# The end of the last batch: bias by a product, residual straight from PSUM, normalisation of three quarters on ScalarE

## The chip, the cores and the metric

The kernel runs on one core of a Trainium2 chip. The metric is device time in microseconds (us) of one whole execution; lower is better. In the profile PE is TensorE (matmuls), PEld its weight loads, DVE is VectorE, ACT is ScalarE, POOL is GpSimd and SP the engine that issues nearly all DMAs. A suffix q (SPq, POOLq) is the sequencer of that engine.

## The reference

Two layers are applied to x, of shape 16 batches x 1024 nodes x 256 channels, in 32-bit floats. Layer 0 is an attention over the nodes (4 heads) whose queries are mixed through the adjacency; layer 1 is two graph convolutions. After each comes a layer norm of the input plus the layer's result. What matters here is the end of layer 1:

```python
def _graph_conv(x, adj, w_loop, w_neigh, b):
    loop = jnp.einsum('bnd,dh->bnh', x, w_loop)
    neigh = jnp.einsum('nm,bmh->bnh', adj, jnp.einsum('bnd,dh->bnh', x, w_neigh))
    return loop + neigh + b
h = jax.nn.relu(_graph_conv(x, adj, w1_loop, w1_neigh, b1))
h = jax.nn.relu(_graph_conv(h, adj, w2_loop, w2_neigh, b2))
return (x + h) * 0.5
...
x = _layernorm(x + _L1_gnn_ref(x, adj, ...), axis=-1)
```

Since x + (x + h)/2 is 1.5 (x + h/3), and a layer norm takes out a common factor, the kernel computes x + h/3: the weights w2 and the bias b2 are divided by three once, at the start, and the norm's epsilon is divided by 2.25 (`EPS2`). The input b2 is a row of 256 numbers; in these inputs it is zero, but the kernel adds it like any other.

## The kernel before

A batch is 1024 nodes, kept as 8 tiles of 128 nodes (partitions) by 256 channels. Through the main loop, batch b's attention runs beside the graph convolutions of batches b-1 and b-2 (class `Joined`, which does two convolutions' adjacency products together) and the norm of b-3. Order is written out by hand: each engine executes its instructions in the order in which the Python code emits them (`tc.manual_schedule()`), with semaphores for data and for buffers that are used again. Only the small check behind it (the lines from 1145 on: whether every softmax denominator stayed in range) is put in place by a scheduler. If that check fails, a slower safe version would run; it does not run here.

After the loop, batches 12 to 15 are finished. The last lines of `run()` do, in this order: the norm and store of batch 12, those of batch 13, `c2.last()` and `c2.moments()` for batch 14, and then `c1.ending(...)` for batch 15, into which the rest of batch 14 is put as `aside`.

`ending` (lines 817 to 841) works on quarters: 2 tiles of 128 nodes each, 512 columns. `second` (line 768) forms u, the neighbour sums of h1 with the adjacency, in two halves of 512 nodes: 8 products of 128x512 each, then a copy from PSUM to SBUF on ACT (`uT`, line 777). Quarters 0 and 1 need the first half of u only, and are put into the middle of the second half; quarters 2 and 3 follow it. A quarter in the kernel before is:

- PE, `outer` (lines 782 and 783): per tile one product with `w2n_sb` and one with `w2l_sb`, summed in PSUM, so four products of 128x256 a quarter. An f32 product shows as two MATMUL instructions in the profile (x2).
- DVE, `residual` (lines 787 and 790): z = PSUM + b2 (128x512), then x = max(z, 0) + x.
- DVE, `statistics` (lines 278 and 279): per tile BN_STATS and BN_AGGR, giving mean and variance.
- DVE and POOL, `reciprocal_deviation` (lines 283 and 284): variance + eps, then the power -1/2 on POOL, which works on a 128x2 piece.
- DVE, `leave` of the quarter before (lines 290 and 825): `normalize` subtracts the mean and multiplies, two instructions of 128x256, and SP stores 256 KB to the output.

So the DVE queue reads z, x, statistics, rstd of quarter g, and then the normalisation of quarter g-1; the last quarter's normalisation comes alone at the end. `rstd`, `mv_e` and the PSUM tiles of one bank have two buffers each, so that a quarter uses again what the one two before it used. Batch 14's norm, `finish_aside` (lines 811 and 813), is already done on ACT: a shift of -mean x rstd is made on DVE, and eight activations x rstd + shift (128x256) follow on ACT.

Of the kernel before, what the change touches and what calls it, by code (L numbers as in the profile page):

```python
# [10 lines left out]
F32 = mybir.dt.float32  # L11
I32 = mybir.dt.int32
AF = mybir.ActivationFunctionType
ALU = mybir.AluOpType
# [4 lines left out]
def kernel(  # L19
# [31 lines left out]
    nc = tc.nc  # L51

    B, N, C = x.shape
    P = 128
# [22 lines left out]
    const = ctx.enter_context(tc.tile_pool(name="const", bufs=1))  # L77
    xpool = ctx.enter_context(tc.tile_pool(name="xpool", bufs=3))
    work = ctx.enter_context(tc.tile_pool(name="work", bufs=1))
    small = ctx.enter_context(tc.tile_pool(name="small", bufs=4))  # L80
# [43 lines left out]
    w2n_sb = const.tile([HID, C], F32, name="w2n_sb")  # L124
    b1_sb = const.tile([HID, 1], F32, name="b1_sb")
    b2_sb = const.tile([P, C], F32, name="b2_sb")
# [30 lines left out]
    nc.gpsimd.memset(neg_half, -0.5)  # L157
    ones_sb = const.tile([P, 1], F32, name="ones_sb")
    nc.gpsimd.memset(ones_sb, 1.0)

    fold = const.tile([P, Q, S], F32, name="fold")
    nc.vector.tensor_reduce(fold[:, 0, :], ident.rearrange("p (i k) -> p k i", k=S), AX.X, ALU.add)
# [112 lines left out]
    def statistics(mv, xb, ts_, name):  # L275
        for t in ts_:
            st = small.tile([P, nc.vector.BN_STATS_DIM], F32, tag="st", name=f"st_{name}_{t}")
            nc.vector.bn_stats(st, xb[:, t, :])
            nc.vector.bn_aggr(mv[:, t, :], st)

    def reciprocal_deviation(mv, name, eps, count=NT):
        rstd = small.tile([P, NT], F32, tag="rstd", name=f"rstd_{name}", bufs=2)[:, 0:count]
        nc.vector.tensor_scalar_add(rstd, mv[:, :, 1], eps)
        nc.gpsimd.tensor_tensor(rstd, rstd, neg_half[:, 0:count], ALU.pow)
        return rstd

    def normalize(mv, rstd, xb, count=NT):

        for t in range(count):
            nc.vector.tensor_scalar(xb[:, t, :], xb[:, t, :], mv[:, t, 0:1], rstd[:, t:t + 1],  # L290
                                    op0=ALU.subtract, op1=ALU.mult)
# [407 lines left out]
    class GraphConv:  # L699
# [76 lines left out]
                self.neighbours(j, pu, range(TJ, NT), rows01)  # L776
                nc.scalar.copy(self.uT[:, ts(j, FB)], pu)

        def outer(self, g, per, p2):
            for i in range(per):  # L780
                t = g * per + i
                nc.tensor.matmul(p2[:, ts(i, C)], self.uT[:, ts(t, P)], w2n_sb, start=True, stop=False)  # L782
                nc.tensor.matmul(p2[:, ts(i, C)], self.h1T[:, ts(t, P)], w2l_sb, start=False, stop=True)  # L783

        def residual(self, g, per, p2):
# [31 lines left out]
        def ending(self, dst, rows01, aside):  # L817

            per = FB // C
            parts = []  # L820

            def leave(g, mv, rstd):
                rows = self.x[:, g * per:(g + 1) * per, :]
                normalize(mv, rstd, rows, per)
                nc.sync.dma_start(out=dst[g * per * P:(g + 1) * per * P, :].rearrange("(t p) c -> p t c", p=P), in_=rows)

            def quarter(g):
                p2 = (bank_psum if g % 2 else half_psum)(f"h2e_ps_{g}")
                self.outer(g, per, p2)
                self.residual(g, per, p2)  # L830
                mv = small.tile([P, per, 2], F32, tag="mv_e", name=f"mv_e_{g}", bufs=2)
                statistics(mv, self.x[:, g * per:(g + 1) * per, :], range(per), f"e{g}")
                rstd = reciprocal_deviation(mv, f"e{g}", EPS2, per)
                if parts:
                    leave(*parts.pop())
                parts.append((g, mv, rstd))

            self.second(rows01, lambda: (aside(), quarter(0), quarter(1)))
            quarter(2)
            quarter(3)  # L840
            leave(*parts.pop())

    class Joined:

# [365 lines left out]
```

## Time and profile before

| what | us |
|---|---|
| median of three runs | 2174.52 |
| the three runs | 2174.29, 2174.52, 2175.86 |
| time of the profiled execution | 2174.29 |
| its span (first to last instruction) | 2172.4 |
| PE busy in the span | 2155.6 (99%) |
| DVE busy | 1893.7 (87%) |
| ACT busy | 1027.7 (47%) |
| POOL busy | 368.2 (17%) |
| stretch from the first product of quarter 0 to the last normalisation | 2150.35 to 2167.80 |

The span and the time of the same execution differ by 1.89 us, which lies outside the first and last instruction. The busy shares are of the whole span. The part that the change touches is the last 22 us of it, so shares over the whole say little of it; the chain of waits and the timeline of that stretch say more. In the chain a row is a start time, a length and what ran; "issue" is time in which the engine waited for nothing that the profile shows. In the groups a row is line, engine, operation, output and inputs, shapes, count, busy time, mean time of one in ns, and the idle time just before it.

### The profile page before, as it was taken

To read this page: it belongs to the slowest core of one execution; us is meant where nothing else is said; L and a number is where in the kernel's file an instruction comes from. 1 tells how busy PE (TensorE), PEld (TensorE's weight loads), DVE (VectorE), ACT (ScalarE), POOL (GpSimd) and SP (SyncE) were. 2 spreads that over 40 slices of the span, in tenths; PEclk is the share of its full clock that TensorE was granted. 3 is DMA by queue.
4 is the path that set the end of the run, shared out by engine and by line. 5 is a ranking of instruction groups with operands and counts; after the bars stand their busy time and mean duration, and the time that the engine had idled before them with its cause. 6 is when DMAs were issued, how large, how long until landed. Compare 5 with 4: busy or idle time off the path is not lost.

```text
span 2172.4 us, 23124 instructions
## 1 busy us (share of the span) xinstructions
PE 2155.6 (99%) x8054; PEld 1026.6 (47%) x8054; DVE 1893.7 (87%) x2431; ACT 1027.7 (47%) x1346; POOL 368.2 (17%) x210
## 2 busy tenths in 40 slices
PE   9999999999999999999999999999999999999997
PEld 5344444544444444444444445454454544544354
DVE  4978988898998989989899898999989899898965
ACT  4744545535455453445444454445543445535411
POOL 1011120221303113031120301203022130221021
PEclk9999999999999999999999999999999999999999
DMA  9393563746557374583655626556374653743342
GB/s 230 95 139 116 140 175 89 119 153 122 149 125 144 124 121 155 125 164 102 113 158 130 163 88 114 172 122 155 97 111 166 121 155 113 121 149 82 117 138 96
DMA packets 610619, 286.22 MB, mean 132 GB/s; under 512 B 504640, under 2 KB 569024, under 8 KB 610496
## 3 DMA queue, kind: packets, MB, share of 16 engines
q1 hardware_dynamic: 610224, 284.15, 55.0%
q8 instruction: 65, 1.06, 0.2%
q14 instruction: 58, 0.48, 0.1%
q10 hardware_dynamic: 272, 0.52, 0.1%
HBM read 238.16 MB, written 46.46 MB: 131 GB/s over the span
## 4 chain that ended last, share of the span: by engine, by line
PE 97%; DVE 2%; ACT 0%; DMA 0%; issue 0%; SPq 0%; POOLq 0%; DVEq 0%; POOL 0%
PE s L596 20%; PE av L616 20%; PE hu_ps L875 17%; PE g_ps L549 16%; PE v_ps L363 5%; PE k_ps L408 4%; PE t_ps L714 3%; PE h_ps L782 3%; PE hu_ps L721 2%; PE g_ps L476 2%; PE h_ps L783 2%; DVE acc L605 1%; PE h_ps L736 1%; PE u_ps L765 1%; PE k_ps L353 1%; PE den_ps L628 0%
## 5 line engine op out<-in xcount | busy, mean ns | idle before, releaser
L599 ACT ACTIVATE pr<-s 128x1024 f32<-128x1024 f32 x512 | 476.4, 1054 | 180.0 <-PE s L596 179.9
L605 DVE TENSOR_TENSOR acc<-acc,pr 128x1024 f32<-128x1024 f32 x384 | 494.4, 1288 | 40.7 <-DVE acc L605 0.5
L596 PE MATMUL s<-qT,kT 64*128 64x512 f32 x2048 | 458.8, 598 | 0.7 <-ACT qT L483 0.7
L616 PE MATMUL av<-pr,v 128*64 128x512 f32 x2048 | 453.6, 595 | 0.0
L596 PEld LDWEIGHTS s<-qT,kT 64*128 64x128 f32 x2048 | 191.8, 186 | 237.1 <-ACT pr L599 109.5
L616 PEld LDWEIGHTS av<-pr,v 128*64 128x64 f32 x2048 | 141.4, 137 | 300.0 <-issue 283.9
L329 POOL TENSOR_TENSOR rstd<-rstd,neg_half 128x32 f32<-128x32 f32 x16 | 87.1, 5441 | 1108.6 <-DVE rstd L327 1108.6
L462 ACT ACTIVATE wg<-c_row,c_col 128x1024 f32<-128x1024 f32 x128 | 147.0, 1148 | 73.0 <-DVE accB L607 54.2
L468 DVE SCALAR_TENSOR_TENSOR wg<-wg,adj 128x1024 f32<-128x1024 f32 x128 | 149.9, 1211 | 13.8 <-ACT wg L463 13.8
L875 PE MATMUL hu_ps<-adj,R 128*128 128x512 f32 x360 | 158.3, 596 | 0.0
L463 ACT ACTIVATE wg<-wg 128x1024 f32<-128x1024 f32 x128 | 135.4, 1058 | 4.1
L317 ACT ACTIVATE sq<-xB_a 128x1024 f32<-128x1024 f32 x32 | 33.8, 1057 | 190.0 <-DVE xB_a L312 188.8
L363 PE MATMUL v_ps<-kvw_sb,xT 128*128 128x256 f32 x512 | 120.2, 379 | 0.1
L549 PE MATMUL g_ps<-wg,S 128*128 128x512 f32 x224 | 116.7, 603 | 0.0
L363 PEld LDWEIGHTS v_ps<-kvw_sb,xT 128*128 128x128 f32 x512 | 97.2, 190 | 38.4 <-issue 21.0
L549 PE MATMUL g_ps<-T,S 128*128 128x512 f32 x224 | 114.4, 592 | 0.0
L549 PE MATMUL g_ps<-wg,x 128*128 128x512 f32 x224 | 109.0, 599 | 0.0
L875 PE MATMUL hu_ps<-adjT,t 128*128 128x512 f32 x240 | 105.7, 592 | 0.0
L875 PEld LDWEIGHTS hu_ps<-adj,R 128*128 128x128 f32 x360 | 67.3, 190 | 78.9 <-issue 76.8
L603 DVE TENSOR_TENSOR acc<-pr,pr 128x1024 f32<-128x1024 f32 x64 | 76.9, 1201 | 24.1 <-ACT pr L599 24.1
L607 DVE STREAM_TRANSPOSE accB<-acc 128x1024 f32<-128x1024 f32 x64 | 79.7, 1245 | 3.1
L609 DVE TENSOR_REDUCE den_part<-accB 128x32 f32<-128x1024 f32 x64 | 78.1, 1220 | 2.2
(187 smaller groups left out, 2862.7 us busy)
## 6 DMA issues: line engine op xcount, KB each, us to landing
adj<-in_adj_dram SPq DMA_DIRECT2D x128, 512.0 KB, 4.7
adj<-adjT SPq DMA_DIRECT2D x120, 512.0 KB, 10.2
para<-in_L_gnn_para_dram SPq DMA_DIRECT2D x32, 512.0 KB, 3.5
xB_a<-in_x_dram SPq DMA_DIRECT2D x128, 128.0 KB, 4.2
x1d<-xB_a SPq DMA_DIRECT2D x128, 128.0 KB, 3.4
x<-x1d SPq DMA_DIRECT2D x16, 1024.0 KB, 16.9
xB<-in_x_dram SPq DMA_DIRECT2D x120, 128.0 KB, 4.4
x<-in_x_dram SPq DMA_DIRECT2D x15, 1024.0 KB, 7.3
```

Source lines behind the costliest of these rows:

```text
L329: nc.gpsimd.tensor_tensor(self.rstd, self.rstd, neg_half, ALU.pow)
L363: nc.tensor.matmul(pv[:, ts(i, C)], xT[:, cc, ts(g * per + i, P)], kvw_sb[:, cc, C:2 * C], start=(cc == 0), stop=(cc == NC - 1))
L408: nc.tensor.matmul(dst, self.a[n], self.w[n], start=not again, stop=True, skip_group_check=again)
L462: nc.scalar.activation(wg, self.c_row, AF.Abs, bias=self.c_col[:, t:t + 1], scale=-1.0)
L463: nc.scalar.activation(wg, wg, AF.Tanh, scale=-0.5)
L468: nc.vector.scalar_tensor_tensor(wg, wg, 1.0, self.adj.pop(t), op0=ALU.add, op1=ALU.mult)
L549: nc.tensor.matmul(self.p[n], x_n[:, k, :], w_n, start=(k == 0), stop=(k == TJ - 1))
L596: nc.tensor.matmul(ps[:, ts(s, FB)], self.kT[rows, pair, ts(mt, P)], self.qT[rows, pair, ts(j, FB)], start=True, stop=True)
L599: nc.scalar.activation(pr, ps, AF.Exp)
L605: nc.vector.tensor_add(acc, acc, pr)
L616: nc.tensor.matmul(pav[s * HD:(s + 1) * HD, :], self.v[:, mt, pair * P + s * HD:pair * P + (s + 1) * HD], self.pr[mt][:, ts(s, FB)], start ...
L875: nc.tensor.matmul(dst, self.x[n][:, k, :], half_adj[w][:, k, :] if w else of_rows(rows, k), start=(start and k == 0), stop=(k == TJ - 1), ...
```

## The change

A row of 128 ones (`ones_row`, one partition) is made at the start. In `ending`:

- `outer` is called with `bias=True`: each tile's sum in PSUM begins with a product of the row of ones and the row of b2, contracted over one partition, ahead of the two products it had. That is two more products of 128x256 a quarter, eight in all.
- `residual` is no longer called there. One operation of DVE reads PSUM, takes the maximum with 0 and adds x.
- `leave` has two forms. For quarters 0, 1 and 2 a shift (128x2) is made on DVE, and two activations on ACT form x rstd + shift. Quarter 3 is normalised on DVE as before.

The order of the calls is the same: quarters 0 and 1 within the second half of `second`, `leave` of quarter g-1 behind the statistics of quarter g. `last()` and `residual()` are as they were for all other batches.

```diff
+    ones_row = const.tile([1, P], F32, name="ones_row")
+    nc.gpsimd.memset(ones_row, 1.0)
...
-        def outer(self, g, per, p2):
+        def outer(self, g, per, p2, bias=False):
             for i in range(per):
                 t = g * per + i
-                nc.tensor.matmul(p2[:, ts(i, C)], self.uT[:, ts(t, P)], w2n_sb, start=True, stop=False)
+                if bias:
+                    nc.tensor.matmul(p2[:, ts(i, C)], ones_row, b2_sb[0:1, :], start=True, stop=False)
+                nc.tensor.matmul(p2[:, ts(i, C)], self.uT[:, ts(t, P)], w2n_sb, start=not bias, stop=False)
                 nc.tensor.matmul(p2[:, ts(i, C)], self.h1T[:, ts(t, P)], w2l_sb, start=False, stop=True)
...
-            def leave(g, mv, rstd):
+            def leave(g, mv, rstd, aside=True):
                 rows = self.x[:, g * per:(g + 1) * per, :]
-                normalize(mv, rstd, rows, per)
+                if aside:
+                    shift = small.tile([P, per], F32, tag="shift_e", name=f"shift_e_{g}", bufs=2)
+                    nc.vector.scalar_tensor_tensor(shift, mv[:, :, 0], -1.0, rstd, op0=ALU.mult, op1=ALU.mult)
+                    for i in range(per):
+                        nc.scalar.activation(rows[:, i, :], rows[:, i, :], AF.Identity, bias=shift[:, i:i + 1],
+                                             scale=rstd[:, i:i + 1])
+                else:
+                    normalize(mv, rstd, rows, per)
                 nc.sync.dma_start(out=dst[g * per * P:(g + 1) * per * P, :].rearrange("(t p) c -> p t c", p=P), in_=rows)
...
-                self.outer(g, per, p2)
-                self.residual(g, per, p2)
+                self.outer(g, per, p2, bias=True)
+                rows = self.x[:, g * per:(g + 1) * per, :]
+                nc.vector.scalar_tensor_tensor(rows, p2.rearrange("p (i c) -> p i c", c=C), 0.0, rows,
+                                               op0=ALU.max, op1=ALU.add)
                 mv = small.tile([P, per, 2], F32, tag="mv_e", name=f"mv_e_{g}", bufs=2)
-                statistics(mv, self.x[:, g * per:(g + 1) * per, :], range(per), f"e{g}")
+                statistics(mv, rows, range(per), f"e{g}")
...
-            leave(*parts.pop())
+            leave(*parts.pop(), aside=False)
```

## The prediction

> **What bounds the kernel now.** I read the page's busy times first, then its chain of waits as shares of the whole span, then the chain in order of time for the last 22 us, then the groups of that stretch with shapes kept apart.
>
> ```profile
> PE 2155.6 (99%) x8054; PEld 1026.6 (47%) x8054; DVE 1893.7 (87%) x2431; ACT 1027.7 (47%) x1346; POOL 368.2 (17%) x210
> ...
> PE 97%; DVE 2%; ACT 0%; DMA 0%; issue 0%; SPq 0%; POOLq 0%; DVEq 0%; POOL 0%
> ```
>
> PE is the bound of 97% of the chain. A product put on PE where PE leads is paid in full; one taken from DVE pays only in the 2% where DVE leads. The end shows where that is:
>
> ```profile
> 2153.81 3.45 PE u_ps L765 x8
> ...
> 2157.28 0.59 ACT uT L777
> ...
> 2157.91 0.70 PE h2e_ps L782 x2
> ...
> 2159.95 0.70 DVE z L787
> ...
> 2162.78 0.64 DVE x L290 x2
> 2163.41 0.61 DVE z L787
> ...
> 2164.05 0.70 DVE x L790
> ...
> 2167.06 0.41 DVE x L290
> ```
>
> The stretch has two parts. Up to 2159.92 PE leads: quarters 0 and 1 (from 2150.35), the rest of u, the copy of u on ACT (0.59), quarter 2. From 2159.95 DVE leads: both steps of the residual of quarter 2, its statistics, the normalisation of quarter 1 (0.64), the same for quarter 3, and at 2167.06, after POOL's power, quarter 3's normalisation, which ends at 2167.80. The last store is issued then and the span ends at 2172.4.
>
> ```profile
> L782 PE MATMUL h2e_ps<-w2n_sb,uT 128*128 128x256 f32 x16 | 4.9, 386 | 0.7 <-ACT uT L777 0.7
> L783 PE MATMUL h2e_ps<-w2l_sb,h1T 128*128 128x256 f32 x16 | 4.8, 379 | 0.0
> L813 ACT ACTIVATE x<-x,shift,rstd_g 128x256 f32<-128x256 f32 x8 | 4.0, 588 | 1.1 <-DVE shift L811 1.1
> ...
> L290 DVE TENSOR_SCALAR x<-x,mv_e,rstd_e 128x256 f32<-128x256 f32 x8 | 2.9, 407 | 0.3 <-POOL rstd_e L284 0.3
> L284 POOL TENSOR_TENSOR rstd_e<-rstd_e,neg_half 128x2 f32<-128x2 f32 x4 | 2.9, 716 | 15.8 <-DVE rstd_e L283 15.8
> L790 DVE SCALAR_TENSOR_TENSOR x<-z,x 128x512 f32<-128x512 f32 x4 | 2.8, 693 | 0.1
> L787 DVE TENSOR_TENSOR z<-h2e_ps,b_sb 128x512 f32<-128x512 f32 x4 | 2.8, 690 | 5.0 <-PE h2e_ps L783 5.0
> ```
>
> Here are the prices: z, which reads PSUM, takes 690 ns, x, which reads SBUF, 693. Products overlap, so not the 386 ns but the spacing in the chain counts: 0.43 us a product (two instructions).
>
> [...] the 64-row score products (line 596) have a mean of 598 ns, the 128-row ones of the same width 596. I price a one-row product at 0.43. [...] For 256 elements and two operands [...] the trace has 588; eight take 4.04 us, so two take 0.59 + 0.49 = 1.08.
>
> **The change part by part.** *Quarters 0 and 1 on PE.* Four bias products, 4 x 0.43 = 1.73 us, stand in PE's queue ahead of the rest of u. PE runs there without a gap, so nothing hides them: u ends at 2158.98 in place of 2157.25.
>
> *The copy of u.* On ACT it now stands behind quarter 0's two activations, which wait for shift 0, which on DVE stands behind the statistics of quarter 1. Quarter 1 leaves PE at 2153.81 + 1.73 = 2155.54 (0.43 apiece from 2150.35, twelve products, gives the same). One stage on DVE, from the residual's last step to the end of rstd, takes 2.11 (2164.05 to 2166.16); rstd 1 ends at about 2157.75, shift 0 at 2157.83, the activations run 2157.86 to 2158.94, and u's copy wants ACT at 2159.00. It fits, with 0.06 to spare: cost nothing, up to 1.08 if that cover goes.
>
> *Quarter 2 on PE.* Its first bias product does not need u. The queue gives it the 0.66 us between 2157.25 and 2157.91 in which PE waits for the copy, so it is free; without that wait it costs 0.43. The second is paid: +0.43. Quarter 2 is ready at 2159.92 + 1.73 + 0.43 = 2162.08.
>
> *DVE from there.* Before, 7.11 us pass from 2159.95 to 2167.06. Removed: z of quarter 2 (0.72 with its gap), normalisation 1 (0.64), z of quarter 3 (0.61 seen in the chain). Added: shift 1, a 128x2 operation like the one of line 811, 0.17. The stage of quarter 2 thus lasts 2.11, plus 0.07 (rstd now also waits for ACT, which read that buffer two quarters earlier; the one rstd that has such a wait today, quarter 1's, starts 0.29 after the operation before it, the others 0.22), plus shift 1: DVE is free at about 2164.37. But quarter 3 comes six products after quarter 2, 2.59 us: 2164.67. Before, DVE reached z of quarter 3 at 2163.41 when PE had finished it by about 2161.65; now PE is late by 0.3 and takes the lead again. So quarter 3's residual starts at 2164.70, and then: 2.11 + 0.07 + the copy of the check's result, which the order now puts behind this residual (0.11 in the chain before, between two dependent steps; I take 0.05, 0 to 0.11; its PE product waits only for quarter 1's PSUM tile and ends well within the residual) + 0.90 from the end of rstd over POOL's power to the normalisation. That is 2167.83 against 2167.06: **+0.77**.
>
> *Stores.* Quarter 2's store follows its activations on ACT: shift 2 ends at 2167.0, ACT at 2168.1. Issued there for 0.37, it is off SP when quarter 3's becomes due at about 2168.57. SP has nothing else queued behind these but the end check. The two stores are 0.45 us apart instead of 1.0; in the windows of the trace a store keeps the DMA engines busy for about 1.1 to 1.3 us, from 0.7 to 1.1 after its issue, so they overlap. I take +0.1, 0 to +0.5. The stores of quarters 0 and 1 end long before. Sum: **+0.9**.
>
> *Edits at nothing.* The memset of the row of ones comes on POOL before the identity matrix, while the two memsets for the denominators move behind it. PE's first real work waits for the load of x, which the chain follows until 7.49, against an identity that is there at 1.5. The row moves later SBUF tiles by 512 bytes; see the last rival.
>
> The profiled execution had a span of 2172.4 and a time of 2174.29. So the span becomes 2173.3 and that time 2175.2; the median of the runs lies 0.23 above it: **2175.4**. A change of under 0.2%, 4.35 us, is about what a measurement of this kernel cannot tell from none, and the three runs already span 1.57. The forecast is "no change", some tenths on the slow side.
>
> **The rivals.** *The bias products are nearly free.* If one row makes a product short, PE's +2.16 goes. Then DVE leads all the way: residual 2 starts near 2160.15 (u's copy waits 0.2 for ACT), residual 3 2.3 later, the last normalisation at 2165.6, that is -1.46, with the stores -1.35: 2173.1. Balance is at a price of about 0.32 us a product. For it speaks only that the weights are one row; against it the 598 and 596.
>
> *The copy of u is caught behind ACT.* The spare is 0.06. If shift 0 comes later by a few tenths ([...] a wait on ACT's own queue), u's copy, quarter 2 and all behind it come later by as much; it decides from 0.06 and is capped by 1.08: 2175.9 to 2176.5, with stores that collide fully 2176.9. Against it: ACT is idle between.
>
> *Slower by more than 0.2%: every tile behind the row of ones moves.* The place is PE's whole span: 8054 matmuls; if each takes 0.54 ns longer through another address of its operands, that is 4.35 us, and from there the verdict is slower (2179 and up). No view shows that a time depends on an address; against it, matmuls of one shape on many buffers differ by a few ns in the mean (592 to 603). The same could as well go the other way.
>
> **How the numbers follow.** Forecast 0.58 (own range 2174.7 to 2176.1, from the bounds above and the spread of the runs); cheap bias products 0.14, 2172.9 to 2174.6 as they are free or partly so; copy caught or stores colliding 0.22, 2175.9 to 2177.3; addresses 0.06, two thirds of it slower. From 2173.2 to 2177.2 leaves out half of the second case, the addresses and the top of the third: under 2 in 10. Faster 0.02, within 0.94, slower 0.04.
>
> **What would show it.** The bias products at 0.43 spacing, u's second half ending 1.7 us later, the copy of u starting within 0.1 of that end, residual 3 waiting for PE and not for DVE, the last normalisation about 0.8 later, and the chain on PE up to quarter 3. Wrong are a copy of u that waits for ACT, bias products below 0.32, [...] or a difference that lies before 2150.

## The result, and the profile after

The change made the kernel slower: a median of 2177.9 us over 22 runs against 2173.99 over 22 of the kernel before, ratio 1.0018 with a 95% interval of 1.0012 to 1.0023. The forecast was 2175.4, between 2173.2 and 2177.2; the time lies above that range. (The ratio itself is inside the 0.2% that the prediction took for indistinguishable from no change; with 22 runs of each kernel its interval excludes 1.) Runs of both kernels fall into groups about 1.7 us apart, taken here by their times as executions in which TensorE's clock was not halved, halved once or halved longer some 290 us into the run (last section), so medians of few runs jump by that much, and single executions are compared within a group. Without a halved stretch the medians are 2176.27 and 2172.63, with one 2177.96 and 2174.25, so the change costs 3.6 to 3.7 us. Both profiles have one such stretch, of 3.4 us at a granted clock of 0.50; their spans are 2176.3 and 2172.4.

The page after, busy times and shares of the chain of waits:

```profile
PE 2161.7 (99%) x8070; PEld 1028.2 (47%) x8070; DVE 1887.5 (87%) x2424; ACT 1030.9 (47%) x1352; POOL 369.5 (17%) x211
...
PE 97%; DVE 2%; ACT 0%; DMA 0%; issue 0%; SPq 0%; POOLq 0%; DVEq 0%; POOL 0%
```

DVE lost 6.2 us of busy time, as intended, and PE gained 6.1 with 16 more instructions, eight products; 8 x 0.43 would be 3.4. The chain of waits of the last stretch, in order of time, says where it went (start, length, what; line 785 is the bias product, 786 and 787 are the former 782 and 783, 843 the residual in one operation):

```profile
2150.49 0.62 PE h2e_ps L785 x2
2151.11 0.63 PE h2e_ps L786 x2
2151.74 0.43 PE h2e_ps L787 x2
...
2157.23 3.45 PE u_ps L767 x8
...
2160.70 0.59 ACT uT L779
...
2162.47 0.62 PE h2e_ps L785 x2
2163.09 0.63 PE h2e_ps L786 x2
2163.72 0.43 PE h2e_ps L787 x2
...
2167.56 0.69 DVE x L843
...
2170.61 0.41 DVE x L292
```

A bias product takes 0.62, and the product behind it 0.63 where it took 0.43 before. One bias product thus costs 0.82, not 0.43. Everything up to residual 3 at 2167.56 is now PE's, but for the copy of u on ACT (0.59). In the groups of the stretch, shapes kept apart:

```profile
L786 PE MATMUL h2e_ps<-w2n_sb,uT 128*128 128x256 f32 x16 | 5.6, 431 | 0.1
L785 PE MATMUL h2e_ps<-b_sb,ones_row 1*128 1x256 f32 x16 | 5.6, 426 | 0.0
L787 PE MATMUL h2e_ps<-w2l_sb,h1T 128*128 128x256 f32 x16 | 4.8, 379 | 0.0
...
L832 ACT ACTIVATE x<-x,shift_e,rstd_e 128x256 f32<-128x256 f32 x6 | 3.3, 592 | 14.2 <-DVE shift_e L830 14.2
...
L843 DVE SCALAR_TENSOR_TENSOR x<-h2e_ps,x 128x512 f32<-128x512 f32 x4 | 2.8, 692 | 12.3 <-PE h2e_ps L787 12.3
```

The residual straight from PSUM takes 692 ns, as the form from SBUF did (693): that part is as cheap as forecast. DVE stands idle for 12.3 us ahead of its four residuals, waiting for PE. The timeline shows where the 0.2 us come from (in a shape such as 1*128 the first number is that of contracted rows, the second that of the weights' columns; start, length, engine, operation; in brackets the idle time before it):

```profile
2150.42 0.29 PEld L785 LDWEIGHTS h2e_ps<-b_sb,ones_row 1*128 1x128 f32 x2 [0.76 <-issue]
2150.42 0.69 PE L785 MATMUL h2e_ps<-b_sb,ones_row 1*128 1x256 f32 x2
2151.04 0.30 PEld L786 LDWEIGHTS h2e_ps<-w2n_sb,uT 128*128 128x128 f32 x2 [0.33 <-issue]
2151.04 0.70 PE L786 MATMUL h2e_ps<-w2n_sb,uT 128*128 128x256 f32 x2
2151.36 0.41 PEld L787 LDWEIGHTS h2e_ps<-w2l_sb,h1T 128*128 128x128 f32 x2
2151.58 0.59 PE L787 MATMUL h2e_ps<-w2l_sb,h1T 128*128 128x256 f32 x2
```

The weights of line 787 begin to load 0.22 ahead of their product, behind the running one. Those of 785 and 786 begin together with their product: ahead of them PEld stood idle (0.76 and 0.33), and the load is not hidden. One load of 128x128 weights has a mean of 190 ns in this profile (line 365), which is the size of the surplus. Both are products whose number of contracted rows (1*128, 128*128) differs from the one before.

### The profile page after: what moved, and what is told of

The parts are those of the page before. It is cut to its first block, busy times and chain, and to the rows that moved or that the text cites. A ratio compares the mean times of both kernels' runs of the same rounds, so it can differ in the third digit from the quotient of the medians.

```text
span 2176.3 us, 23157 instructions
## 1 busy us (share of the span) xinstructions
PE 2161.7 (99%) x8070; PEld 1028.2 (47%) x8070; DVE 1887.5 (87%) x2424; ACT 1030.9 (47%) x1352; POOL 369.5 (17%) x211
## 4 chain that ended last, share of the span: by engine, by line
PE 97%; DVE 2%; ACT 0%; DMA 0%; issue 0%; SPq 0%; POOLq 0%; DVEq 0%; POOL 0%
PE s L598 20%; PE av L618 20%; PE hu_ps L889 17%; PE g_ps L551 16%; PE v_ps L365 5%; PE k_ps L410 4%; PE t_ps L716 3%; PE h_ps L786 2%; PE hu_ps L723 2%; PE g_ps L478 2%; PE h_ps L787 2%; DVE acc L607 1%; PE h_ps L738 1%; PE u_ps L767 1%; PE k_ps L355 1%; PE den_ps L630 0%
## 5 line engine op out<-in xcount | busy, mean ns | idle before, releaser
L905 ACT COPY snap<-hu_ps 128x512 f32<-128x512 f32 x15 | 8.8, 586 | 150.4 <-PE hu_ps L889 150.4
```

## The experiments

Positions are taken from each run's chain of waits and counted from the start of quarter 0's first product, so that they do not depend on what lies before. "Last norm" is where the last normalisation starts; "end" is from there to the span's end; times are medians of runs without and with one halved stretch (told by their times), as differences from the kernel before in the same group, run on the same chip. Some of these groups hold only two to four runs. Taken over all runs without groups, the interval of the ratio includes 1 for e1, e4, e7, e8, e9 and e10, so the small differences rest on the groups and on the positions.

| run | last norm | end | without | with one |
|---|---|---|---|---|
| before | 16.71 | 5.4 | 0 | 0 |
| the change | 20.12 | 5.7 | +3.6 | +3.7 |
| e1_rows128 | 17.39 | 5.7 | +1.0 | +1.0 |
| e2_rows64 | 20.13 | 5.8 | +3.7 | +3.7 |
| e3_wide | 18.42 | 5.8 | +2.1 | +2.0 |
| e4_no_bias | 14.87 | 6.7 | -0.8 | -0.8 |
| e5_aside_only | 17.88 | 5.8 | +1.5 | +1.4 |
| e6_no_aside | 20.08 | 5.5 | +3.4 | +3.6 |
| e7_late_bias | 15.25 | 5.7 | -1.4 | -1.0 |
| e8_pieces | 15.27 | 5.6 | -1.2 | -1.1 |
| e9_no_bias_late_dve | 14.91 | 6.6 | -1.1 | -1.0 |
| e10_two_tiles | 14.55 | 5.5 | -2.1 | -2.0 |

**Is it the one row, the border between row numbers, or any third product?** Theory S was that a product with another number of rows than its forerunner cannot load its weights ahead; the rivals were that one row is slow in itself (R) and that any third product costs this much (A). Three runs tell them apart. First, 128 rows in the bias product:

```diff
-    ones_row = const.tile([1, P], F32, name="ones_row")
-    nc.gpsimd.memset(ones_row, 1.0)
+    ones_row = const.tile([128, P], F32, name="ones_row")
+    nc.gpsimd.memset(ones_row, 1.0 / 128)
...
-nc.tensor.matmul(p2[:, ts(i, C)], ones_row, b2_sb[0:1, :], start=True, stop=False)
+nc.tensor.matmul(p2[:, ts(i, C)], ones_row, b2_sb[0:128, :], start=True, stop=False)
```

> The changed kernel with the bias product contracted over 128 rows (a matrix of 1/128 against all 128 copies of b2) in place of one row; nothing else differs. Theory S (a product whose stationary operand has another number of rows than the one before it cannot load its weights ahead, which exposes about 0.2 us at each of the two borders of a one-row product): the borders are gone, bias products and those behind them are spaced 0.43, u's second half ends near 2159.0 and the last normalisation starts near 2167.9; the time is 0.8 to 1.1 above before and 2.8 to 3.1 below the change. Rival R (one row read from one partition is slow in itself): the same here. Rival A (any third product in the group costs 0.82, whatever its rows, for its start flag or for the extra weights): 0.62 and 0.63 remain and the time is that of the change, 3.9 above before.

Its chain:

```profile
2150.50 0.43 PE h2e_ps L785 x2
2150.93 0.43 PE h2e_ps L786 x2
2151.36 0.43 PE h2e_ps L787 x2
...
2155.68 3.45 PE u_ps L767 x8
```

All products are spaced 0.43; the time is 1.0 above before, which is where my working had put the change itself. In the kernel before, at the same place and also with 128 rows on both sides, the weights of line 782 begin to load at 2149.76, 0.43 ahead of their product at 2150.19, where those of line 785 in the change begin with it:

```profile
2149.76 0.19 PEld L782 LDWEIGHTS h2e_ps<-w2n_sb,uT 128*128 128x128 f32 x1 [0.24 <-issue]
...
2150.19 0.59 PE L782 MATMUL h2e_ps<-w2n_sb,uT 128*128 128x256 f32 x2
```

A falls. The median of all its runs (2175.13 against 2172.97) has a ratio of 1.0004 with an interval of 0.9995 to 1.0012; the difference within a group is clearer.

Second, 64 rows, the same edit with 64 for 128:

> As the run with 128 rows, but contracted over 64 rows (1/64 each). Theory S: 64 rows differ from 128 as one row does, so the bias product takes 0.62 and the one behind it 0.63, and the time is that of the change, 3.7 to 4.1 above before. Rival R (slow because of one row): 0.43 or close to it, time 0.8 to 1.5 above before. Rival A: 0.62 and 0.63 as in the change.

```profile
2150.48 0.63 PE h2e_ps L785 x2
2151.11 0.63 PE h2e_ps L786 x2
2151.74 0.43 PE h2e_ps L787 x2
```

With 64 rows it is as slow as with one, so R falls: the single row is not the reason. What 1 and 64 rows have in common is that they differ from the 128 of the products on both sides, and the product behind, which has 128 rows, is late as well. Third, the same one-row work with half the borders:

```diff
+            if bias:
+                nc.tensor.matmul(p2[:, 0:per * C].rearrange("p (i c) -> p i c", c=C), ones_row,
+                                 b2_sb[0:1, :].unsqueeze(1).to_broadcast([1, per, C]), start=True, stop=False, skip_group_check=True)
             for i in range(per):
...
-                if bias:
-                    nc.tensor.matmul(p2[:, ts(i, C)], ones_row, b2_sb[0:1, :], start=True, stop=False)
```

> The changed kernel with one one-row product of 512 columns a quarter in place of two of 256. Theory S: two borders a quarter in place of four; the wide product takes 0.86 + 0.2, the one behind it 0.63, all others 0.43; u ends 0.8 earlier than in the change (near 2159.9), the bias of quarter 2 stands wholly in the wait for u's copy, and the time is 1.1 to 1.6 below the change. Rival R (a one-row product takes 0.62 for 256 columns by its own speed): the wide one takes 1.24 or more, u ends at most 0.4 earlier, the time is 0.4 to 0.8 below the change.

```profile
2150.49 1.05 PE h2e_ps L783 x2
2151.54 0.63 PE h2e_ps L787 x2
2152.17 0.43 PE h2e_ps L788 x2
2152.60 0.43 PE h2e_ps L787 x2
```

The wide product takes 1.05 = 0.86 + 0.19, the one behind it 0.63, the second of its kind 0.43. R had asked for 1.24 or more. Four borders a quarter have become two, and the time fell by 1.6 to 1.7, at or just above the upper end of what S said (1.6) and above what R said. S stands in all three.

**What the other parts are worth.** Without any bias product (`self.outer(g, per, p2)` in place of `..., bias=True)`; b2 is left out):

> The changed kernel without the bias products, so b2 is left out; residual in one operation and normalisation on ACT stay. If PE's extra products are the whole loss: u ends at 2157.25 as before, quarter 2's residual starts near 2160.2, the last normalisation near 2165.6, time 1.2 to 1.5 below before (5 below the change). If part of the loss lies in the ACT or the one-operation residual: at or above before.

The last normalisation comes 1.84 earlier than in the kernel before, more than the 1.46 that I had worked out; but the time is only 0.8 lower, not 1.2 to 1.5, and the stretch behind it is 6.7 long instead of 5.4. The last run of this section goes after that. So the whole loss of the change lies in the bias products, and the rest, taken together, is a gain.

The normalisation on ACT alone, put into the kernel before (`leave` as in the change, residual and outer as before):

> The kernel before with only the normalisation of quarters 0 to 2 moved to ACT; bias and residual on DVE in two steps as before. Theory Q (order on ACT): quarter 0's two activations wait for a shift that stands behind quarter 1's statistics on DVE, end near 2159.0, and the copy of u, which stands behind them on ACT, starts 1.6 to 1.8 later than before; DVE then saves 0.5 on the normalisation of quarter 1, so the last normalisation comes 1.1 to 1.3 later and the time is 1.2 to 1.7 above before. Rival (the move to ACT relieves DVE and nothing waits): the copy of u is not late and the time is 0.4 to 0.7 below before.

```profile
2156.26 0.07 DVE shift_e L826
2156.33 0.02 issue
2156.36 1.09 ACT x L828 x2
2157.45 0.48 ACT uT L777
```

The copy of u, which feeds quarter 2, is caught behind two activations and starts 8.69 after quarter 0 in place of 6.93, as theory Q said: +1.5 in time. In the change itself this does not happen, since u is late there anyway: the copy starts 0.02 after u ends. The opposite, the change with every quarter normalised on DVE (`aside=False` as the default of `leave`):

> The changed kernel with all four quarters normalised on DVE as before; one-row bias products and the one-operation residual stay. Theory S (PE leads all the way to quarter 3): DVE has 1.1 to spare ahead of residual 3 and more ahead of residual 2, so the two instructions put back cost nothing, the last normalisation stays within 0.1 of the change's, and the stores are about 1 apart again: time 0 to 0.4 below the change. Rival (the move to ACT is what keeps the change from losing more): 0.6 or more above the change.

The last normalisation starts 20.08 after quarter 0 against 20.12: ACT's part is worth nothing there, because DVE waits for PE in front of each residual. The times agree to 0.2.

**A version that keeps the gain and not the loss.** Keep the parts that pay where they pay: quarters 0 and 1 as before, since DVE has room and PE has none; one wide bias product over 128 rows for quarters 2 and 3, where quarter 2's falls into PE's wait for u; ACT for quarter 1 alone.

```diff
-    ones_row = const.tile([1, P], F32, name="ones_row")
-    nc.gpsimd.memset(ones_row, 1.0)
+    ones_row = const.tile([P, P], F32, name="ones_row")
+    nc.gpsimd.memset(ones_row, 1.0 / P)
...
+            if bias:
+                nc.tensor.matmul(p2[:, 0:per * C].rearrange("p (i c) -> p i c", c=C), ones_row,
+                                 b2_sb.unsqueeze(1).to_broadcast([P, per, C]), start=True, stop=False, skip_group_check=True)
...
-                self.outer(g, per, p2, bias=True)
+                fast = g >= 2
+                self.outer(g, per, p2, bias=fast)
...
+                if fast:
+                    nc.vector.scalar_tensor_tensor(rows, p2.rearrange("p (i c) -> p i c", c=C), 0.0, rows,
+                                                   op0=ALU.max, op1=ALU.add)
+                else:
+                    self.residual(g, per, p2)
...
-                    leave(*parts.pop())
+                    leave(*parts.pop(), aside=(g == 2))
```

> Quarters 0 and 1 as in the kernel before (bias and residual in two steps, normalisation of quarter 0 on DVE); quarters 2 and 3 with one bias product of 512 columns over 128 rows each and the residual in one operation; only quarter 1 normalised on ACT. Theory S with the path worked out: u's second half ends where it did before, the bias product of quarter 2 (0.86) fills PE's wait for the copy of u, quarter 2 is ready within 0.1 of before, residual 3 starts 0.9 earlier than before's second step of it less z, and the last normalisation 1.3 to 1.6 earlier than before; with the stores 1 apart the time is 1.2 to 1.6 below before. If stores or another wait eat it: 0 to 0.5 below.

```profile
2155.27 3.43 PE u_ps L767 x8
2158.70 0.86 PE h2e_ps L783 x2
2159.56 0.52 PE h2e_ps L787 x2
```

The last normalisation starts 1.46 earlier than in the kernel before; median of all runs 2171.38 against 2173.95, ratio 0.9992, 0.9984 to 1.0000; within the groups it is 1.0 to 1.4 below. The same working, with the price of the product put right, had forecast 1.3 to 1.6 for the normalisation, which holds, and 1.2 to 1.6 for the time, which holds in one group and not in the other. Next, u's second half was also formed in two pieces of 256 columns, with z kept in quarter 2:

```diff
-                fast = g >= 2
+                fast = g == 3
...
-            self.second(rows01, lambda: (aside(), quarter(0), quarter(1)))
+            self.uT = row_tile(f"uT_{self.b}")
+            pu = half_psum(f"u_ps_{self.b}_0")
+            self.neighbours(0, pu, range(NT), rows01)
+            nc.scalar.copy(self.uT[:, 0:FB], pu)
+            pu = big_psum(f"u_ps_{self.b}_1")
+            H = FB // 2
+            def piece(h, mts):
+                for mt in mts:
+                    nc.tensor.matmul(pu[:, h * FB:h * FB + H], self.h1[:, ts(mt, P)],
+                                     adj_block(mt // TJ, 1, mt % TJ, rows01)[:, ts(h, H)],
+                                     start=(mt == 0), stop=(mt == NT - 1))
+            piece(0, range(TJ))
+            piece(1, range(TJ))
+            aside()
+            quarter(0)
+            quarter(1)
+            for h in range(2):
+                piece(h, range(TJ, NT))
+                nc.scalar.copy(self.uT[:, FB + h * H:FB + (h + 1) * H], pu[:, h * FB:h * FB + H])
```

> As the run with late bias products, but the second half of u is formed in two pieces of 256 columns (in two PSUM banks), so that the copy of the first piece runs while PE forms the second, and quarter 2 keeps z and adds b2 on DVE; the bias product remains in quarter 3 alone. PE should run from the first product of quarter 0 to the end of quarter 3 with no wait; quarter 2 ready 0.8 to 1.0 earlier than before, last normalisation 1.7 to 2.1 earlier, time 1.6 to 2.1 below before. If products of 256 columns cannot hide their weight loads: each of the 16 costs up to 0.2 more and the time is at or above before.

This missed: the normalisation comes 1.44 earlier, not 1.7 to 2.1, and the time is 1.1 to 1.2 lower, not 1.6 to 2.1. The chain has a wait of PE for the copy of the first piece, 0.45 in all, which no data asks for:

```profile
2152.23 1.74 PE u_ps L866 x8
2153.97 0.02 issue
2153.99 0.38 ACT uT L877
2154.37 0.04 issue
2154.42 1.99 PE u_ps L866 x8
```

The two pieces lay in one PSUM tile, in columns 0 to 255 and 512 to 767. With a tile for each (`pus = [half_psum(...)[:, 0:FB // 2] for h in range(2)]`):

> As the run with u in two pieces, but each piece has a PSUM tile of its own, so that the products of the second piece need not wait for the copy of the first. If that wait (0.45 in the chain) is from the shared tile: PE runs without a gap, quarter 2 is ready 0.4 to 0.5 earlier than there, the last normalisation starts 1.8 to 2.0 earlier than in the kernel before and the time is 1.5 to 1.9 below before. If PE needs the wait for another reason: as there, 1.1 to 1.3 below before.

```profile
2153.95 3.45 PE u_ps L866 x16
2157.41 0.43 PE h2e_ps L787 x2
```

No gap, and the last normalisation comes 2.16 earlier than in the kernel before, somewhat more than forecast (1.8 to 2.0). Median of all runs 2172.19 against 2174.08, ratio 0.9993, 0.9984 to 1.0001, an interval that includes 1; within the groups it is 2.0 to 2.1 below (forecast 1.5 to 1.9).

**The long end without bias products.** Quarter 2's normalisation was put back on DVE (`aside=(g < 3)`), so that its store goes out about 1 before the last one:

> As the run without bias products (b2 left out), but quarter 2 is normalised on DVE again, during POOL's power, so that its store is issued about 1 before the last one and not 0.4. Theory T (two stores close together delay the last one): the last normalisation starts within 0.1 of the run without bias products, and the stretch from its end to the span's end shrinks from 5.9 to 4.6 to 5.0; time 0.8 to 1.3 below that run. Rival (the long stretch there was chance or has another cause): the stretch stays at 5.5 or more and the time within 0.3.

The stretch stayed 6.6 from the last normalisation's start: theory T fell. In the windows of that run the share of the DMA engines stays at 0.05 to 0.08 for 2 us after the bulk of the stores (2168.5 to 2170.5). Without bias products alone it is at 0.06 to 0.13 for 1.5 us (2166.5 to 2168), but so it is with the normalisation on ACT alone (0.04 to 0.13, 2170 to 2171.5), where the end is 5.8; in the kernel before, the change and the runs over 128 rows and with two tiles such a stretch lasts at most 0.75 us. Why the end is longer in the two kernels without bias products stays open.

## Why the prediction was wrong

By its own steps, in us on the path from quarter 0 to the last normalisation, against the kernel before (there residual 2 begins with z, and residual 3 is the second of its two steps, at 2164.05):

| step | forecast | measured |
|---|---|---|
| four bias products ahead of u's end | +1.73 | +3.29 |
| end of u to residual 2 | +0.43 | +0.81 |
| residual 2 to residual 3 | -1.51 | -0.73 |
| residual 3 to last normalisation | +0.12 | +0.04 |
| sum | +0.77 | +3.41 |
| stores and end | +0.1 | +0.35 |

- **The step that failed** is "I price a one-row product at 0.43". It measured 0.62, and the product behind it 0.20 more: 0.82. The surplus of 0.39, four times, once and twice, is 2.73; the first three rows differ from the forecast by 1.56, 0.38 and 0.78, together 2.72.
- That price was my estimate, and the 598 and 596 ns which I gave for it are means over long rows of products of one shape, where no border shows. They are also lengths of instructions that overlap, not the spacing that the prediction says counts: by spacing, the score products of line 596 (64*128) and those of line 875 (128*128), both 512 wide, differ, with 0.22 an instruction (12 in 2.58, below; the kernel issues them in pairs, on rows 0 to 63 and 64 to 127) against 0.43:

```profile
2129.27 3.43 PE hu_ps L875 x8
```

  So these two means could not support the price. The kernel before does show borders; I did not look there. In its chain of waits at one of them, from the products of line 616 (128*64) to those of line 782 (128*128):

```profile
1002.71 2.58 PE s L596 x12
1005.29 7.02 PE av L616 x32
1012.30 0.63 PE h_ps L782 x2
1012.93 0.43 PE h_ps L783 x2
1013.36 0.43 PE h_ps L782 x2
```

  The first product behind the change of shape takes 0.63, its sisters 0.43: the surplus of one border, in a profile that was at hand. (Here the number of columns changes, not that of rows.)
- The bounds of that price were set on the wrong side only: the rival asked what happens if the product is cheaper (balance at 0.32, and it turned out dearer). The rest of the mechanism was right: PE takes the lead, quarter 3 waits for PE, the bias product ahead of u's copy is hidden in the wait. With 0.43 a product, as in the run over 128 rows, the sum comes out: +0.7 on the path (17.39 against 16.71) and +1.0 in time, for +0.77 and +0.9.
- The one-operation residual at the price of the SBUF form, the activations at 1.08 a pair (1.09 measured), and the copy of the check's result at next to nothing (0.05 in the chain) were right. One sum is off without effect: with the 0.17 that it names for shift 1, DVE would be free at 2164.46, not 2164.37, still before 2164.67.
- Rival "copy caught behind ACT": it did not occur in the change, where u ended only after quarter 0's activations had (2160.68 against 2160.63). Both wait for PE, so the dearer product moved them together, and the forecast spare of 0.06 came out at 0.05. It is real where u is on time: with ACT alone +1.5 in time, and without bias products a copy that starts 7.13 after quarter 0 in place of 6.93, the 0.2 that the prediction gave for that case.
- Rival "every tile moves by 512 bytes": no sign of it. Quarter 0's first product starts at 2150.49 against 2150.35, and runs that have the row of ones differ among themselves by as much.
- Stores: I gave 0.1 and blamed their distance. The end grew by 0.35, but it is 5.5 to 5.8 in most runs whatever the distance, so the cause that I gave is not shown.

## What to carry to other kernels

Read the price of an added product at the place where it will stand: a product with another number of rows than its neighbours paid here for its weight load and for that of the next, 0.2 us each, together nearly as much again as its own 0.43, and one border where the columns change showed the same 0.2. If a bias must go through TensorE, give it the row number of its neighbours (all products spaced 0.43 in the run over 128 rows), one wide product in place of two (two borders a quarter in place of four, 1.6 to 1.7 less in time), and a place in a wait (with late bias u ended 6.89 after quarter 0's first product, in the kernel before 6.90). And move work away from an engine only where that engine leads: in the kernel before PE led up to 2159.95 and DVE after it, and a bias product lost in the one half and gained in the other.

## What the runs showed of the hardware

- In the change the weights were not loaded ahead over a change of the row number: those of the one-row product behind one with 128 rows, and those of the 128-row product behind it, began to load with their product (2150.42 and 2151.04), and each border cost 0.19 to 0.20 us. With 64 rows beside 128 the products were spaced 0.63 and 0.63, the same surplus; with 128 beside 128 they were spaced 0.43, without a surplus.
- A clock dip behind a wait of PE. At about 286 us PE waits 2.3 us for a sum on DVE in the kernel before (2.32), the change (2.31), the run without bias products (2.33) and the one with late bias (2.32). Behind it TensorE's granted clock falls to 0.50 for 3.4 us in the kernel before and in the change, and for 6.8 with late bias; without bias products it stays at 1.00. In the kernel before and in the change no other stretch with PE at work shows a fall. The times of these four executions lie in the lowest group of their kernel without the dip (2171.90), in the next, 1.7 higher, with 3.4 us of it (2174.29 and 2178.20), and in the third with 6.8 (2174.50); for the other executions the group is inferred from this. Windows of the kernel before, a run with a dip (window, length, busy us of PE, PEld, DVE, ACT, POOL, granted clock, DMA share, GB/s):

```profile
286.00:287.00 1.00, 0.00 (x0) 0.00 (x0) 0.97 (x2) 0.87 (x1) 0.77 (x1) 1.00 1.30 86
287.00:288.00 1.00, 0.00 (x0) 0.00 (x0) 1.00 (x1) 0.00 (x0) 0.99 (x1) 1.00 1.20 25
...
290.00:291.00 1.00, 1.00 (x6) 0.48 (x4) 0.97 (x2) 0.68 (x1) 1.00 (x1) 0.50 0.94 89
...
294.00:295.00 1.00, 1.00 (x6) 0.39 (x4) 1.00 (x2) 1.00 (x2) 0.00 (x0) 1.00 0.39 12
```

  The run without bias products has the same wait and no dip. That the wait brings the dip about is not shown, and what decides whether the clock falls was not tried; but its 1.7 us are nearly as much as the best version here gained.
